# Normalizing and transposing the first layernorm's tokens in 32 by 32 blocks on VectorE instead of through TensorE

## The chip, the core and the metric

The kernel runs on one core of a Trainium2 chip. The metric is the device time of one execution in microseconds (us). Below, PE is TensorE's matmul stream, PEld its weight loads, DVE is VectorE, ACT is ScalarE, POOL is GpSimd, and SP is the engine that issues most DMAs. A DMA that is issued from SP, ACT or POOL stands in that engine's instruction stream, in order with its other instructions.

## What is computed

Four batches of 512 tokens with 512 features (x), and 1024 context rows for each batch. All numbers are float32.

```python
x = x + xattn(layernorm(x), ctx)     # linear attention, 16 heads of 32, feature map elu+1, sigmoid gate
x = x + moe(layernorm(x))            # 8 experts of 512x512, each token goes to its best 2

# layernorm: (x - mean) / sqrt(var + 1e-5) over the features, no scale or shift
# xattn:  q = f(query @ Wq.T); gate = sigmoid(query @ Wg.T + bg); k, v = split(kv @ Wkv.T); k = f(k)
#         out = ((q @ sum_s(k v)) / (q . sum_s(k) + 1e-6) * gate) @ Wo.T,  f(a) = a + 1 if a > 0 else exp(a)
# moe:    logits = x @ Wr; top 2; softmax over the two; sum of gate * (x @ We[e] + be[e])
```

The change concerns the first layernorm, the one ahead of the attention.

## The kernel before

Tokens come in tiles of 128 (`NT` = 4 for each batch), context rows in tiles of 128 (`NS` = 8 for each batch), and features in `NC` = 4 chunks of 128. A projection multiplies with the features on the 128 partitions, so the normalized tokens must be transposed: `xT` holds features on partitions and tokens along the row. For a tile, `normalized_T` (L248) normalizes into `xn` on DVE, and `transposed` (L241) makes four TensorE transposes of 128x128 into the PSUM tile `pt` and copies it to SBUF on ACT. The second layernorm's tokens (`row`, in `choose`, L471) go the same way into `x2T`, for the router's logits `pl`.

`layernorm_stats` (L225) makes mean and variance of each token with two DVE instructions for a tile, then the root on ACT and the reciprocal on DVE for four tiles at once. The result has a token on each partition.

The order of the work:

- `kv_tiles(b, lo, hi)` (L321) walks a batch's context tiles: for each, keys (`pk`: 8 matmuls; minimum on DVE, exponential on ACT, `k` by a second DVE instruction), values (`pv`: 8 matmuls, copied by ACT into `v`, whose last column a POOL memset fills with ones), and `kv_add`, which adds the tile before to the sums `kvs` (8 shorter matmuls). Two callbacks put other work in: `inside` after the first keys, `between` after each tile.
- Batch 0: three context tiles, the statistics of `x`, then five more, with `normalized_T` of one token tile between each of the first four.
- For each batch b: four projections for the queries (`pq`), with `dispatch(b - 1)` in the middle, then the gates (`pg`), the attention products (`pz`, `pn`), four context tiles of batch b + 1, the output projection (`po`, added to `x` on DVE), and the other four context tiles of batch b + 1. Between these last four, `normalized_T` of batch b + 1 and the next step of `choose(b)` take turns.
- `dispatch(b)` (L519) scatters each token's `row` to two places of the DRAM tensor `stream`, with eight indirect DMAs from POOL. Tokens are kept there by expert.
- Instead of a further batch, batch 3 has the first of the experts: `run` (L677) loads tiles of 128 rows from `stream` (`xg`, in blocks of 32 tokens by 128 features, four DMAs from SP, and `of`, two numbers for each token), transposes them 32 by 32 on DVE (`turned`, L721), multiplies (`pe`, 8 matmuls with one expert's weights), adds the bias into `y`, and scatters `y` to the DRAM tensor `result` (POOL, L757). Expert weights are loaded in this block layout too, so that a 32 by 32 transpose within partition groups is enough. 17 tiles are early ones and 18 late ones (steps 0 to 17; `SURE` = 18).
- At the steps of a plan (`begins`, `at_step`), `fetch` (L810) reads a token tile's rows of `result` back from POOL, `add` combines them with `x`, and `store` writes the output. The tiles fall in five groups; the first fetch of a group loads a row number into a register of POOL. The last two token tiles (14, 15) are read by SP and ACT after the last step.

The compiler's scheduler may reorder instructions of an engine within their dependencies. `tc.keep_in_program_order(i)` pins `i` behind the one instruction that was traced just ahead of it on its engine, and `mark()` (L455) writes a one-element tile on POOL with such a pin; successive marks also write the same bytes and so keep their order. A write to `result` is pinned behind its own mark. In `fetch`, the mark stands after the register load.

SP's loads are in program order. `cT` (context tiles) has three buffers, shared with `xg`; `row` has four, one for each token tile. `xT` is one buffer that each batch takes anew. `set_empty` fills `stream` with empty rows from SP, 1 MB at a time, during the first batches.

Of the kernel before, what the change touches and what calls it, by code (L numbers as in the profile page):

```python
# [9 lines left out]
F32 = mybir.dt.float32  # L10
# [3 lines left out]
ALU = mybir.AluOpType  # L14
# [3 lines left out]
P = 128  # L18
B, L, S, D = 4, 512, 1024, 512
E, F = 8, 512  # L20
HD = 32
NC = D // P
NT = L // P
NS = S // P
# [7 lines left out]
ROW = D + 2  # L32
# [7 lines left out]
SURE = LATE - 4  # L40
# [13 lines left out]
def xattn_moe_kernel(  # L54
# [14 lines left out]
    nc = tc.nc  # L69
# [9 lines left out]
    work = ctx.enter_context(tc.tile_pool(name="work", bufs=2))  # L79
    small = ctx.enter_context(tc.tile_pool(name="small", bufs=2))  # L80
    pmm = ctx.enter_context(tc.tile_pool(name="pmm", bufs=6, space=PSUM))
    pkv = ctx.enter_context(tc.tile_pool(name="pkv", bufs=1, space=PSUM))
    dram = ctx.enter_context(tc.tile_pool(name="dram", bufs=1, space=DRAM))
# [3 lines left out]
    result = dram.tile([NOWHERE + 2 * L, F], F32, name="result")  # L87


    def matmul(**operands):  # L90
        tc.keep_in_program_order(nc.tensor.matmul(**operands))  # L91

# [4 lines left out]
    latest = {}  # L97

    def load(dst, src):
        latest["load"] = nc.sync.dma_start(out=dst, in_=src)  # L100
        tc.keep_in_program_order(latest["load"])

    def load_ctx(b, s):
# [2 lines left out]
        load(t, cT[b, s])  # L106
        return t

    def load_x(b):
        tiles = []  # L110
        for t in range(NT):
            xt = xpool.tile([P, D], F32, tag="x", name=f"x_{b}_{t}")
            load(xt, x[b, t])
            tiles.append(xt)
        return tiles

    wkv_sb = wpool.tile([P, NC, 2 * D], F32, tag="wkv", name="wkv_sb")
    wq_sb = wpool.tile([P, NC, D], F32, tag="wq", name="wq_sb")
    wg_sb = wpool.tile([P, NC, D], F32, tag="wg", name="wg_sb")
    wo_sb = wpool.tile([P, NC, D], F32, tag="wo", name="wo_sb")  # L120
    wr_sb = wpool.tile([P, NC, E], F32, name="wr_sb")
    bg_sb = wpool.tile([P, NC], F32, name="bg_sb")


    we_sb = wpool.tile([P, E, NC, F], F32, name="we_sb")
    we_rows = we.rearrange("e (c f) i n -> e i f c n", f=HD)

# [14 lines left out]
    xs = {0: load_x(0)}  # L142

    turned = [(g, 0, g * HD, P - g * HD) for g in range(NC)]
    turned += [(g, P - g * HD, 0, g * HD) for g in range(1, NC)]
    wg_in = big.tile([P, NC, D], F32, tag="aT", name="wg_in")
    load(wg_in, wg)
    for g, a, b, n in turned:
        nc.gpsimd.tensor_copy(
            wg_sb[:, :, g * P + b : g * P + b + n], wg_in[:, :, g * P + a : g * P + a + n]  # L150
        )
        load(bg_sb[b : b + n, g : g + 1], bg[a : a + n, g : g + 1])
    load(wq_sb, wq)
    load(wr_sb, wr)
    for g, a, b, n in turned:
        load(wo_sb[b : b + n, g, :], wo[a : a + n, g, :])


    ident = const.tile([P, P], F32, name="ident")
# [18 lines left out]
    for g in range(NC):  # L178
        r = slice(g * HD, (g + 1) * HD)
        for i in range(NC):  # L180
            o = (i + g) % NC
            nc.gpsimd.affine_select(
                out=spread[r, o, :], in_=spread[r, o, :], pattern=[[0, HD]],
# [34 lines left out]
    def feature_map(dst, src):  # L218

        ex = work.tile([P, D], F32, tag="ex", name="ex")  # L220
        nc.vector.tensor_scalar(ex, src, 0.0, None, ALU.min)  # L221
        nc.scalar.activation(ex, ex, AF.Exp)  # L222
        nc.vector.scalar_tensor_tensor(dst, src, 0.0, ex, ALU.max, ALU.add)  # L223

    def layernorm_stats(tiles):  # L225
        mv = small.tile([P, NT, 2], F32, tag="mv", name="mv")
        for t in range(NT):
            st = small.tile([P, 6], F32, tag="st", name="st")
            nc.vector.bn_stats(st, tiles[t])
            nc.vector.bn_aggr(mv[:, t, :], st)  # L230
        rstd = small.tile([P, NT], F32, tag="rstd", name="rstd")
        nc.scalar.activation(rstd, mv[:, :, 1], AF.Sqrt, bias=eps_sb)
        nc.vector.reciprocal(rstd, rstd)
        return mv, rstd

    def normalize(dst, xt, t, mv, rstd):
        nc.vector.tensor_scalar(
            dst, xt, mv[:, t, 0:1], rstd[:, t : t + 1], ALU.subtract, ALU.mult
        )

    def transposed(dst, src):  # L241

        pt = pmm.tile([P, NC, P], F32, tag="mm", name="pt")
        for c in range(NC):
            transpose(pt[:, c, :], src[:, ts(c, P)])
        nc.scalar.copy(dst, pt)

    def normalized_T(xT, t, tiles, mv, rstd):  # L248

        xn = work.tile([P, D], F32, tag="ex", name="xn")  # L250
        normalize(xn, tiles[t], t, mv, rstd)
        transposed(xT[:, :, ts(t, P)], xn)

    def new_xT():
        return big.tile([P, NC, L], F32, tag="xT", name="xT")
# [199 lines left out]
    def mark():  # L455

        tc.keep_in_program_order(nc.gpsimd.memset(marked, 0.0))
# [13 lines left out]
    def choose(b, mv, rstd):  # L471

        pl = pmm.tile([P, NT, E], F32, tag="mm", name="pl")
        rows, xTs = [], []
        for t in range(NT):
            row = work.tile([P, ROW], F32, tag="row", name="row", bufs=NT)
            normalize(row[:, 0:D], xs[b][t], t, mv, rstd)
            nc.gpsimd.tensor_copy(row[:, D : D + 1], home[:, b * NT + t : b * NT + t + 1])
            rows.append(row)

        def logits(t):
            for c in range(NC):
                matmul(
                    out=pl[:, t, :],
                    lhsT=xTs[t][:, c, :],
                    rhs=wr_sb[:, c, :],
                    start=(c == 0),
                    stop=(c == NC - 1),
                )

        for t in range(NT):
            xTs.append(work.tile([P, NC, P], F32, tag="z", name="x2T"))
            transposed(xTs[t], rows[t])
            if t > 0:
                logits(t - 1)
            yield
        logits(NT - 1)
        lg = small.tile([P, NT, E], F32, tag="lg", name="lg")
        nc.vector.tensor_copy(lg, pl)

        def largest(name):
            m = small.tile([P, NT, 1], F32, tag=f"m{name}", name=f"m{name}")
            hot = small.tile([P, NT, E], F32, tag=f"hot{name}", name=f"hot{name}")
            at = small.tile([P, NT, 1], F32, tag=f"at{name}", name=f"at{name}")
            nc.vector.tensor_reduce(m, lg, AX.X, ALU.max)
            nc.vector.tensor_tensor(hot, lg, m.to_broadcast([P, NT, E]), ALU.is_equal)
            nc.vector.tensor_tensor(hot, hot, rank, ALU.mult)
            nc.vector.tensor_reduce(at, hot, AX.X, ALU.max)
            nc.vector.tensor_tensor(hot, hot, at.to_broadcast([P, NT, E]), ALU.is_equal)
            return m, hot, at  # L510

        m1, hot1, first = largest("1")
        nc.vector.scalar_tensor_tensor(lg, hot1, -BIG, lg, ALU.mult, ALU.add)
        m2, hot2, _ = largest("2")

        routed[b] = rows, m1, hot1, first, m2, hot2
        yield
# [292 lines left out]
    def fetch(t, tiles, queue, group=None):  # L810

        pool, tag = homes[t // 2 % len(homes)]
        if t not in fetched:
            pair = pool.tile([P, 2, 2, F], F32, tag=tag, name=f"y_{t}")
            fetched[t], fetched[t + 1] = pair[:, 0], pair[:, 1]
        if group is None:
            src = flat[:, t]
        else:
            if group not in rows_of:
                rows_of[group] = nc.values_load(  # L820
                    spots[0:1, group : group + 1], [queue.engine], min_val=0, max_val=NOWHERE,
                    skip_runtime_bounds_check_because="one of two constants",
                )
            row = rows_of[group] + (t - READ[group][0]) * 2 * P
            src = result[ds(row, 2 * P), :].rearrange("(p i) f -> p i f", i=2)
        mark()
        load = queue.dma_start(out=fetched[t], in_=src)
        behind(load, written["result"][:tiles], "results of the tokens")
        for put in written["result"][tiles:]:
            tc.declare_no_dep(load.ins, put.ins, reason=read_again)  # L830
        tc.keep_in_program_order(load)
        read_back.append(load)
# [31 lines left out]
    def plan(step, *what):  # L864
        at_step.setdefault(min(step, SURE), []).append(what)

    begins = (-3, -2, -1, 0, 5, 6, 7, 8, 10, 11, 14, 15, SURE - 1, SURE - 1)
    for g, (lo, hi, most) in enumerate(READ):
        for t in range(lo, hi):
            plan(begins[t], fetch, t, most, nc.gpsimd, g)  # L870
# [9 lines left out]

    xT = new_xT()
    kv_tiles(0, 0, 3)
    ln = layernorm_stats(xs[0])
    kv_tiles(0, 3, NS, lambda i: i < NT and normalized_T(xT, i, xs[0], *ln))
    kv_blocks(sums[0])
    for b in range(B):
        more = b + 1 < B
# [42 lines left out]
        next(product)  # L930
        if more:
            xs[b + 1] = load_x(b + 1)
            kv_tiles(b + 1, 0, NS // 2, inside=lambda: next(product))
        else:
            next(early)
            next(product)
            for _ in range(3):
                next(early)
        attention_out(b, aT)
        choice = choose(b, *layernorm_stats(xs[b]))  # L940
        if more:
            ln = layernorm_stats(xs[b + 1])
            xT = new_xT()

            def between(i):
                normalized_T(xT, i, xs[b + 1], *ln)
                next(choice)

            kv_tiles(b + 1, NS // 2, NS, between)
            next(choice)  # L950
            kv_blocks(sums[b + 1])
    for _ in range(2):
# [124 lines left out]
```

## Time and profile before

| what | value |
|---|---|
| median of 3 runs | 621.65 us (619.83 to 622.51) |
| profiled execution | 622.61 us, span 621.0 us |
| mean granted TensorE clock | 0.983 of full speed |
| PE / DVE / ACT / POOL busy | 588.5 / 271.0 / 115.2 / 100.6 us |
| DMA | 105.55 MB, 170 GB/s over the span |
| end of the last matmul | 597.3 us |

A line of instructions reads: source line, engine, operation, the tile written and the tiles read, shapes, and times. "L91" is the helper through which all matmuls go, "L94" the transposes, so groups are told apart by tile names. In a timeline a line has the start, the duration, the engine, and in brackets how long the engine sat idle before it and what ended that. In the list of an instruction's times the three numbers are the least, the median and the largest in ns. Matmuls are pipelined: their durations overlap, and starts tell how much of the stream one takes.

### The profile page before, as it was taken

What the parts mean: (1) busy time and instruction counts of PE and PEld (TensorE: products, weight loads), DVE (VectorE), ACT (ScalarE), POOL (GpSimd) and SP (SyncE); (2) the same over time, 40 slices, a digit from 0 to 9 for tenths busy, and PEclk for the clock granted to TensorE, in tenths of its full rate; (3) what the DMA queues carried; (4) which work ended last, traced back from release to release, by engine and by line L of the source; (5) the groups of instructions that cost most, each with busy time, mean ns of one, the idle gap of its engine ahead of it and who ended that gap; (6) DMA issues with size and microseconds to landing.
All of it is one profiled execution on the core that took longest, in us unless ns stands there. A gap on an engine that the chain in (4) does not pass through costs nothing. (4 is left out here: it accounts for less than half of the span.)

```text
span 621.0 us, 6578 instructions
## 1 busy us (share of the span) xinstructions
PE 588.5 (95%) x1908; PEld 286.3 (46%) x1908; DVE 271.0 (44%) x668; ACT 115.2 (19%) x180; POOL 100.6 (16%) x274
## 2 busy tenths in 40 slices
PE   7999999999999999999999999999999999999940
PEld 3555543454565335446643454565434554443410
DVE  2222243216215341351454226127874569475663
ACT  1322222112322221142222211322210100000000
POOL 4100000000002200000050000002311227455540
PEclk9999999999999999999999999999999999999985
DMA  8648920682686227527530660933344444889965
GB/s 317 191 158 301 293 81 2 167 240 69 164 248 184 81 86 237 153 85 221 186 137 1 203 204 0 327 130 137 116 114 119 96 119 177 262 243 259 296 219 173
DMA packets 68597, 105.55 MB, mean 170 GB/s; under 512 B 11981, under 2 KB 30413, under 8 KB 68176
## 3 DMA queue, kind: packets, MB, share of 16 engines
q1 hardware_dynamic: 58944, 76.24, 41.7%
q0 software_dynamic: 8176, 26.78, 12.1%
q10 hardware_dynamic: 1440, 2.10, 1.1%
q8 instruction: 16, 0.26, 0.2%
q14 instruction: 21, 0.17, 0.1%
HBM read 45.93 MB, written 59.94 MB: 170 GB/s over the span
## 5 line engine op out<-in xcount | busy, mean ns | idle before, releaser
L91 PE MATMUL pk<-wkv_sb,cT 128*128 128x512 f32 x256 | 118.6, 607 | 4.4 <-DMA cT<-in_cT_dram 4.4
L91 PE MATMUL pv<-wkv_sb,cT 128*128 128x512 f32 x256 | 115.2, 593 | 0.0
L221 DVE TENSOR_SCALAR ex<-pk 128x512 f32<-128x512 f32 x32 | 22.0, 688 | 148.3 <-PE pk L91 148.3
L91 PEld LDWEIGHTS pv<-wkv_sb,cT 128*128 128x128 f32 x256 | 48.4, 190 | 62.3 <-issue 59.3
L91 PEld LDWEIGHTS pk<-wkv_sb,cT 128*128 128x128 f32 x256 | 47.7, 194 | 57.8 <-issue 49.9
L91 PE MATMUL pe<-we_sb,xgT 128*128 x144 | 62.8, 595 | 0.6 <-DVE xgT L721 0.6
L91 PE MATMUL pe<-we_sb,turned_rows 128*128 x136 | 60.3, 597 | 0.7 <-DVE turned_rows L721 0.7
L278 POOL MEMSET v<- 128x4 f32 x32 | 3.3, 105 | 345.3 <-PE kvs L91 282.3
L91 PE MATMUL pg<-xT,wg_sb 128*128 128x512 f32 x128 | 56.7, 596 | 0.0
L91 PE MATMUL pq<-xT,wq_sb 128*128 128x512 f32 x128 | 56.6, 596 | 0.0
L91 PE MATMUL po<-wo_sb,aT 128*128 128x512 f32 x128 | 55.6, 592 | 0.0
L222 ACT ACTIVATE ex<-ex 128x512 f32<-128x512 f32 x48 | 30.2, 630 | 136.2 <-DVE ex L221 126.6
L757 POOL DMA_INDIRECT result<-y,to x35 | 35.8, 1023 | 93.7 <-DVE y L753 88.4
L91 PEld LDWEIGHTS pe<-we_sb,xgT 128*128 128x128 f32 x144 | 27.0, 190 | 36.3 <-issue 29.9
L91 PEld LDWEIGHTS pe<-we_sb,turned_rows 128*128 128x128 f32 x136 | 25.3, 190 | 32.4 <-issue 29.5
L563 POOL DMA_INDIRECT stream<-row,slot x32 | 31.9, 996 | 50.3 <-DVE cmp L591 22.5
L91 PEld LDWEIGHTS kvs<-v,k 128*128 128x128 f32 x256 | 33.3, 191 | 13.4 <-issue 13.4
L91 PEld LDWEIGHTS pg<-xT,wg_sb 128*128 128x128 f32 x128 | 24.0, 190 | 32.1 <-issue 32.1
L91 PEld LDWEIGHTS po<-wo_sb,aT 128*128 128x128 f32 x128 | 24.1, 190 | 29.2 <-issue 28.7
L91 PEld LDWEIGHTS pq<-xT,wq_sb 128*128 128x128 f32 x128 | 23.8, 190 | 27.3 <-issue 27.3
L91 PE MATMUL kvs<-v,k 128*128 128x129 f32 x256 | 34.0, 275 | 0.0
L223 DVE SCALAR_TENSOR_TENSOR k<-pk,ex 128x512 f32<-128x512 f32 x32 | 22.1, 690 | 19.5 <-ACT ex L222 19.5
(175 smaller groups left out, 465.1 us busy)
## 6 DMA issues: line engine op xcount, KB each, us to landing
stream<-empty SPq DMA_DIRECT2D x24, 1028.0 KB, 8.1
stream<-empty SPq DMA_DIRECT2D x8, 1285.0 KB, 6.8
xg<-stream SPq DMA_DIRECT2D x140, 64.0 KB, 2.7
we_sb<-in_we_dram SPq DMA_DIRECT2D x32, 256.0 KB, 5.5
cT<-in_cT_dram SPq DMA_DIRECT2D x31, 256.0 KB, 3.1
y<-result POOLq DMA_DIRECT2D x14, 512.0 KB, 5.5
x<-in_x_dram SPq DMA_DIRECT2D x16, 256.0 KB, 6.6
out_dram<-y POOLq DMA_DIRECT2D x10, 256.0 KB, 4.6
```

The lines of the kernel that those rows point to most:

```text
L91: tc.keep_in_program_order(nc.tensor.matmul(**operands))
L221: nc.vector.tensor_scalar(ex, src, 0.0, None, ALU.min)
L222: nc.scalar.activation(ex, ex, AF.Exp)
L223: nc.vector.scalar_tensor_tensor(dst, src, 0.0, ex, ALU.max, ALU.add)
L278: nc.gpsimd.memset(v[:, :, P : P + 1], 1.0)
L563: put = nc.gpsimd.indirect_dma_start(out=stream, out_offset=bass.IndirectOffsetOnAxis(ap=slots[i][:, t, :], axis=0), in_=rows[t], in_offse ...
L757: put = nc.gpsimd.indirect_dma_start(out=result, out_offset=bass.IndirectOffsetOnAxis(ap=home_i, axis=0), in_=y, in_offset=None, bounds_ch ...
```

## The change

The first layernorm's tokens are loaded a second time, in blocks (`load_blocks`): partition i x 32 + t holds, for each of the 16 groups of 32 tokens of a batch, the i-th 128 features of the group's token t. They are normalized in place, four DVE instructions of 128x128 for a token tile, and one DVE instruction transposes the tile 32 by 32 into `xT`. The weights `wq` and `wg` are loaded so that the feature order fits (`load_rows`, four DMAs instead of one). Mean and reciprocal root, which the statistics leave on the partitions of whole tokens, are written to the DRAM tensor `moments` by two POOL DMAs and read back to the blocks' partitions by four more (`spread_moments`). `tc.issue_after(latest["map"].ins)` queues the normalization on DVE behind the latest `k`.

The blocks take the buffer of the four `row` tiles, which become one tile of the same size. For batches 1 to 3 the statistics and the normalization move from the second four context tiles to the first four. `wo` is loaded after the first three context tiles instead of before them. In `fetch`, a `mark()` stands ahead of the register load, and token tiles 12 and 13 are read back at step `SURE - 2` instead of `SURE - 1`.

```diff
+    moments = dram.tile([B, HD, NT, P // HD, 2], F32, name="moments")
...
+    def load_blocks(b):
+        blocks = work.tile([P, NT, ROW], F32, tag="row", name="blocks", bufs=1)
+        blocks = blocks.rearrange("p t r -> p (t r)")[:, 0 : NT * D]
+        for i in range(NC):
+            load(
+                blocks[ts(i, HD), :].rearrange("t (n f) -> t n f", f=P),
+                x[b, :, :, ts(i, P)].rearrange("k (j t) f -> t (k j) f", t=HD),
+            )
+        return blocks
...
+    def load_rows(dst, w):
+        for i in range(NC):
+            load(dst[ts(i, HD)], w.rearrange("(c f) i n -> i f c n", f=HD)[i])
...
-    load(wg_in, wg)
+    load_rows(wg_in, wg)
...
-    load(wq_sb, wq)
+    load_rows(wq_sb, wq)
+    blocks = load_blocks(0)
     load(wr_sb, wr)
-    for g, a, b, n in turned:
-        load(wo_sb[b : b + n, g, :], wo[a : a + n, g, :])
...
-        nc.vector.scalar_tensor_tensor(dst, src, 0.0, ex, ALU.max, ALU.add)
+        latest["map"] = nc.vector.scalar_tensor_tensor(dst, src, 0.0, ex, ALU.max, ALU.add)
...
-    def normalized_T(xT, t, tiles, mv, rstd):
-        xn = work.tile([P, D], F32, tag="ex", name="xn")
-        normalize(xn, tiles[t], t, mv, rstd)
-        transposed(xT[:, :, ts(t, P)], xn)
+    def spread_moments(b, tiles):
+        mv, rstd = layernorm_stats(tiles)
+        for k, of in enumerate((mv[:, :, 0], rstd)):
+            nc.gpsimd.dma_start(
+                out=moments[b, :, :, :, k].rearrange("t n j -> j t n"), in_=of
+            )
+        ln = small.tile([P, NT, P // HD, 2], F32, tag="ln", name="ln", bufs=1)
+        for i in range(NC):
+            nc.gpsimd.dma_start(
+                out=ln[ts(i, HD)].rearrange("t n j k -> t (n j k)"),
+                in_=moments[b].rearrange("t n j k -> t (n j k)"),
+            )
+        return ln
+
+    def normalized_T(xT, t, blocks, ln):
+        rows = blocks[:, ts(t, D)].rearrange("p (j f) -> p j f", f=P)
+        with tc.issue_after(latest["map"].ins):
+            for j in range(P // HD):
+                nc.vector.tensor_scalar(
+                    rows[:, j], rows[:, j], ln[:, t, j, 0:1], ln[:, t, j, 1:2],
+                    ALU.subtract, ALU.mult,
+                )
+            nc.vector.transpose(
+                xT[:, :, ts(t, P)].rearrange("p c (j t) -> p j c t", t=HD),
+                rows.rearrange("p j (c f) -> p j c f", f=HD),
+            )
...
+        batch = work.tile([P, NT, ROW], F32, tag="row", name="rows", bufs=1)
         for t in range(NT):
-            row = work.tile([P, ROW], F32, tag="row", name="row", bufs=NT)
+            row = batch[:, t, :]
...
             if group not in rows_of:
+                mark()
                 rows_of[group] = nc.values_load(
...
-    begins = (-3, -2, -1, 0, 5, 6, 7, 8, 10, 11, 14, 15, SURE - 1, SURE - 1)
+    begins = (-3, -2, -1, 0, 5, 6, 7, 8, 10, 11, 14, 15, SURE - 2, SURE - 2)
...
     kv_tiles(0, 0, 3)
-    ln = layernorm_stats(xs[0])
-    kv_tiles(0, 3, NS, lambda i: i < NT and normalized_T(xT, i, xs[0], *ln))
+    for g, a, b, n in turned:
+        load(wo_sb[b : b + n, g, :], wo[a : a + n, g, :])
+    ln = spread_moments(0, xs[0])
+    kv_tiles(0, 3, NS, lambda i: i < NT and normalized_T(xT, i, blocks, ln))
...
             xs[b + 1] = load_x(b + 1)
-            kv_tiles(b + 1, 0, NS // 2, inside=lambda: next(product))
+            blocks = load_blocks(b + 1)
+            xT = new_xT()
+            def between(i):
+                if i == 0:
+                    ln.append(spread_moments(b + 1, xs[b + 1]))
+                else:
+                    for t in {1: (0,), 2: (1,), 3: (2, 3)}[i]:
+                        normalized_T(xT, t, blocks, ln[0])
+            ln = []
+            kv_tiles(b + 1, 0, NS // 2, between, inside=lambda: next(product))
...
         if more:
-            ln = layernorm_stats(xs[b + 1])
-            xT = new_xT()
-            def between(i):
-                normalized_T(xT, i, xs[b + 1], *ln)
-                next(choice)
-            kv_tiles(b + 1, NS // 2, NS, between)
+            kv_tiles(b + 1, NS // 2, NS, lambda i: next(choice))
```

## The prediction

> **What bounds the kernel now.** I read the page first: engine shares and the 40 slices.
>
> ```profile
> span 621.0 us, 6578 instructions
> ...
> PE 588.5 (95%) x1908; PEld 286.3 (46%) x1908; DVE 271.0 (44%) x668; ACT 115.2 (19%) x180; POOL 100.6 (16%) x274
> ...
> PE   7999999999999999999999999999999999999940
> ...
> PEclk9999999999999999999999999999999999999985
> ```
>
> TensorE is busy in every slice until the last two, at an unreduced clock; VectorE and ScalarE have room. So TensorE's stream sets when the tail begins, and what is taken out of it comes off one for one, if nothing new is late. Next the instructions on the tile pt, and TensorE's timeline in the second half of batch 1's context tiles.
>
> ```profile
> L94 PE MATMUL pt<-ident,xn x64: 272/273/328, 37.3 to 417.8; 128*128 128x128 f32 x64
> ...
> L246 ACT COPY xT<-pt x16: 586/586/587, 37.9 to 418.1; 128x512 f32<-128x512 f32 x16
> ```
>
> ```profile
> 147.14 3.60 PE L91 MATMUL pk<-wkv_sb,cT 128*128 128x512 f32 x8
> ...
> 154.00 1.06 PE L91 MATMUL kvs<-v,k 128*128 128x129 f32 x8
> 156.00 0.66 PE L94 MATMUL pt<-ident,xn 128*128 128x128 f32 x4 [0.94 <-DVE xn L237]
> 156.50 0.60 PE L94 MATMUL pt<-ident,row 128*128 128x128 f32 x4
> 156.93 3.60 PE L91 MATMUL pk<-wkv_sb,cT 128*128 128x512 f32 x8
> 160.37 3.60 PE L91 MATMUL pv<-wkv_sb,cT 128*128 128x512 f32 x8
> 163.80 1.06 PE L91 MATMUL kvs<-v,k 128*128 128x129 f32 x8
> 164.69 0.60 PE L94 MATMUL pt<-ident,xn 128*128 128x128 f32 x4
> 165.13 0.60 PE L94 MATMUL pt<-ident,row 128*128 128x128 f32 x4
> 165.57 0.96 PE L91 MATMUL pl<-wr_sb,x2T 128*128 128x8 f32 x8
> ```
>
> Matmuls overlap, so starts are what to subtract: the four transposes of a tile take 165.13 - 164.69 = 0.44 us of TensorE, not 4 x 0.27. And the first of them waits for its tile (bracket, 0.94); kvs to pt is 2.00 us where at 163.80 it is 0.89, so 1.11 us are lost. The same wait stands at 272.88 and 389.76. Last the end of the POOL timeline, and the chain that ended last.
>
> ```profile
> 592.02 0.55 POOL L851 DMA_DIRECT2D out_dram<-y  x1 [1.28 <-DVE y L840]
> ...
> 598.18 1.02 POOL L757 DMA_INDIRECT result<-y,to  x1 [0.27 <-DVEq L1012]
> ...
> 600.06 0.56 POOL L827 DMA_DIRECT2D y<-result  x1 [0.64 <-issue]
> ...
> 600.71 0.55 POOL L827 DMA_DIRECT2D y<-result  x1
> 604.72 1.03 POOL L757 DMA_INDIRECT result<-y,to  x1 [3.46 <-issue]
> ```
>
> ```profile
> 592.02 11.38 DMA out_dram<-y
> ...
> 604.72 2.33 DMA result<-y,to
> 607.30 6.38 DMA y<-result
> ```
>
> TensorE ends at 597.3; the last expert tile y is ready at 598.04, but its write leaves only at 604.72, after two reads that the program has behind it, and after the store of 592.02, the eighth POOL transfer before it, has landed (592.02 + 11.38 = 603.40). The last two read-backs start when that write has landed, at 607.05.
>
> **TensorE's part.** Sixteen tiles lose four transposes: 16 x 0.44 = 7.0 us, all in the full stream. The stall before the first transpose goes three times: 3 x 1.11 = 3.3, together 10.3. What is late next there is the transpose of row, now first. Its row (152.1 to 152.7 now, behind eight statistics) is behind four afterwards; TensorE asks at 154.9. No new stall. Checked by periods from pk to pk: the first is 156.93 - 147.14 = 9.79 and would be 7.75 + 0.44 = 8.19, so 1.60 less; the other three lose 0.44 each; three batches of 2.92 and batch 0's 4 x 0.44 make 10.5, which I take. ScalarE loses 16 copies of 0.59, off the path.
>
> By the Trainium skill, VectorE: DVE Perf Modes, The three transpose paths, one transpose of 128x128 (bf16) takes 390 ns on TensorE, and Rules for kernel authors gives such transposes to TensorE. By its 390 ns the 64 would save 25 us and the sum would read about 595; the rows here show 0.11 us each on the stream, and the trace decides.
>
> **VectorE's part.** A tile costs four subtract-and-scale on 128x128 and one transpose. The transpose of 128x512 is there: 0.70 (L721). 128x128 lies between 0.16 (L579, 128x4) and 0.54 (L237, 128x512): on the line between, 0.25. So 4 x 0.25 + 0.70 = 1.7 us a tile (1.3 to 2.9), against 0.54 removed. In the four first tiles of a batch (101.9 to 133.4) VectorE is busy 9.8 of 31.5 us; 4 x 1.7 and four statistics of 0.87 make it 20.1. Hidden, unless it waits.
>
> **The round trip over DRAM**, the open cost. After map(0) ends at 109.4, statistics 3.5, table load and root 1.28 + 0.30, reciprocal 0.17: moments ready at 114.7. POOL issues two writes of 512 four-byte runs; no such row is there. Bounds: 0.58 each (L827) to 4 x 0.97 = 3.9 (L563 has 128 rows); I take 1.0, since most of L563's 0.97 is shared by L827 with its larger rows. Landing: 3.2 (scatters of stream, 1.6 to 14.0). Four reads at 0.58 and a gap of 0.3: 3.6; landing 2.4 (of<-stream, 1.6 to 5.1). So ln lands at 114.7 + 2.0 + 3.2 + 3.6 + 2.4 = 125.9. The first normalization stands on VectorE behind map(1) (115.9) and waits; behind it stand the minimum, then the maximum, of k(2). The one waiting for those is kvs(2) at 132.5. Back from there 1.7 for the tile, 0.69 for the minimum, 0.76 for the exponential between, 0.69 for the maximum: ln must land by 128.7. Margin 2.8 us; each us beyond costs TensorE one us in each of three batches. Where the scheduler puts k(2) first, or the statistics into VectorE's idle 7.5 us before 101.2, the margin is larger. On POOL only the memset of v waits behind (118.19 now), used by the same kvs(2). I take nothing.
>
> The Trainium skill, DMA: Bandwidth & Descriptors, Specifications, holds that writes under 512 B become read-modify-writes, which speaks against these; its Anatomy of one DMA gives 2.0 us fixed for a POOL transfer. With 2.0 for both landings ln would be at 124.3; no run yet shows four-byte writes.
>
> **Loads.** Blocks are 1 MB a batch. At the start they replace wo's 1 MB in SP's order; six more weight loads and four block loads at some 0.45, less seven of wo (4.3 us), put cT(0,3) at 22.3 + 4.5 - 4.3 = 22.5. It lands 3.1 later (at most 5.0): 27.5, needed at 29.5. For batches 2 and 3 the block load waits on SP for the scatters of the batch before, whose rows share its buffer: the last leaves at 205.3, lands near 209. Behind it wait cT, expert weights and fills; the next cT is needed at 234.6, the blocks (8.9 at most for x, so 218) at about 232. Cost nothing; without that cover, one us per us. For batch 1 the load (68) falls into full DMA slices and has until 115. wo is needed at 133.
>
> **The tail.** With mark ahead of the register load, a write can no longer slip behind a group's first read; two reads move a step up. POOL's order becomes write 14, read 10, store, write 15, read 11, store, write 16, read 12, read 13, write 17. Read 12 waits until write 15 (595.6) lands at the median 3.9: 599.5; with register loads 0.9 and two issues, write 17 leaves at 601.6. The eighth transfer before it is now read 10 (about 593.9 + 5.5 = 599.4), done. Landing 3.9 (2.3 to 6.8): 605.5, against 607.05. Gain 1.5, between -1.4 and, if it could leave right behind write 16 at 599.3 and land in 2.3, 5.4.
>
> **Sum.** 10.5 + 1.5 = 12.0. The profiled execution took 622.61, 1.6 outside its span, so 610.6; it is 0.96 above the median 621.65, so the median becomes 609.7.
>
> **Rivals.** *Slower: the moments come too late.* If POOL pays by the descriptor (3.9 a write) and the reads land in 5.1, ln is at 114.7 + 7.8 + 3.2 + 3.6 + 5.1 = 134.4: 5.7 us too late, 3 x 5.7 = 17, time 627. It decides at a trip of 14.0 us; the gain is gone at 14.0 + 12.0/3 = 18.0; slower by 0.5% (3.1 us) from 19.0. For it: the margin is thin and landings reach 14.0. Against: short runs here (of, 8 bytes) land in 2.4. *Partly late:* 2 us three times, and no tail gain: 617. *The tail keeps its place or worse:* write 17 bound by the landing of write 15 at its longest 6.8: 611 to 612.5. *VectorE or SP becomes the bound at the start:* cT(0,3) late by up to 4: 614. *The stream does not shorten* (the compiler fills it with waits elsewhere): 621.
>
> **Numbers.** Forecast 0.65 (606 to 613), tail kept 0.08, start late 0.05, partly late 0.07: faster 0.85. Gain eaten by the trip or not there: 0.06. Late moments in full: 0.09. The range runs from about 605.7 (10.5 + 5.4 off) to 618 (10.5 off, tail -1.4 and 2 late in each of three batches: 618.5), leaving out some 0.15. About 0.5% is what a measurement of this kernel can tell from no change.
>
> **What would show it.** Right: no pt<-ident,xn; 9.0 us from pk to pk in the second half of a batch's tiles, 8.2 in its first; TensorE ending 10 us earlier; the last write of result some 3.5 us behind the one before (6.5 now), the last reads some 8 us behind TensorE's end instead of 10. Wrong: kvs waiting for k or v in tiles 1 to 3 of batches 1 to 3, VectorE idle on ln; pk waiting for cT near 30; a late write 17.

## The result, and where the time went

The changed kernel takes 625.98 us (median of 8 executions, 624.15 to 629.58) against 621.56 us for the kernel before (8 executions): ratio 1.0092, 95% interval 1.0074 to 1.0110. It is slower, by some 4.4 us in the medians; 609.7 was predicted. The profiled execution is one of the longer ones of its kernel (629.0 us, span 627.4). So below the trace tells where the time went, and the medians and ratios how much.

The page of the changed kernel, its shares and two of its rows in 40 slices (in this kernel's views L94 is the helper of all matmuls and L103 that of all loads from SP):

```profile
span 627.4 us, 6573 instructions
...
PE 583.6 (93%) x1844; PEld 280.3 (45%) x1844; DVE 291.0 (46%) x732; ACT 107.4 (17%) x164; POOL 122.5 (20%) x303
...
PE   7849999999999999999999999999999999998940
...
PEclk9959999999999999999999999999999999999985
```

TensorE has 64 matmuls less, as intended, but a hole in the third slice (31 to 47 us), and the granted clock falls there to half. After that it is at nine tenths or more up to the last two slices, as in the kernel before. Starts of landmarks on TensorE's timeline put the whole account in one table; pz is the first product of a batch's attention, so it comes once a batch.

| start of | before | after | difference | change since the row above |
|---|---|---|---|---|
| pz of batch 0 | 99.85 | 112.24 | +12.39 | +12.39 |
| pz of batch 1 | 216.73 | 226.21 | +9.48 | -2.91 |
| pz of batch 2 | 333.61 | 340.18 | +6.57 | -2.91 |
| pz of batch 3 | 450.71 | 454.37 | +3.66 | -2.91 |
| first pe from xgT (experts) | 533.91 | 537.55 | +3.64 | -0.02 |
| TensorE's end | 597.31 | 602.88 | +5.57 | +1.93 |
| end of the span | 621.0 | 627.4 | +6.4 | +0.83 |

The lines behind the first two rows, from the timelines of TensorE, before and then after, each with the fourth context tile's keys ahead of them:

```profile
29.53 3.60 PE L91 MATMUL pk<-wkv_sb,cT 128*128 128x512 f32 x8
...
99.85 1.14 PE L91 MATMUL pz<-z,spread 32*128 32x512 f32 x8
...
216.73 1.14 PE L91 MATMUL pz<-z,spread 32*128 32x512 f32 x8
```

```profile
40.67 6.58 PE L94 MATMUL pk<-wkv_sb,cT 128*128 128x512 f32 x8 [11.37 <-DMA cT<-in_cT_dram]
...
112.24 1.14 PE L94 MATMUL pz<-z,spread 32*128 32x512 f32 x8
...
226.21 1.14 PE L94 MATMUL pz<-z,spread 32*128 32x512 f32 x8
```

The gain is there, 2.91 us in each of three batches. It is paid away before the first pz, and a little more in the last two rows. The start, in the chain of waits of the changed kernel (start, duration, what):

```profile
11.70 7.94 DMA wg_in<-in_wg_dram
...
19.66 8.64 DMA wq_sb<-in_wq_dram
...
28.31 5.61 SPq L103
...
34.03 6.59 DMA cT<-in_cT_dram
...
40.67 6.58 PE pk L94 x8
```

The last piece of wg_in lands at 19.64, and only then does SP send the first piece of wq_sb; when that lands, at 28.30, SP goes on with wr_sb, whose issue takes 5.61 us; then cT(0,3), the fourth context tile, leaves, lands at 40.62, and the keys start. TensorE had stood idle for 11.37 us and then does the 8 matmuls in 6.58 us instead of 3.60. Together these are 14.35 us; less the 1.76 us of batch 0's transposes, 12.6, within 0.2 of the first row of the table.

Between the wg_in piece and wq_sb stand the seven loads of bg_sb; between the first piece of wq_sb and wr_sb stand three more pieces and four block loads. In both places a load left when the eighth load before it had landed, as if SP had eight places for loads under way. But the wait for a place is not all. SP's timeline in the changed kernel:

```profile
19.66 2.25 SPq L103 DMA_DIRECT2D wq_sb<-in_wq_dram  x4
21.95 5.63 SPq L103 DMA_DIRECT2D blocks<-in_x_dram  x4
28.31 5.61 SPq L103 DMA_DIRECT2D wr_sb<-in_wr_dram  x1
```

SP stood idle for only 0.73 us before wr_sb (27.58 to 28.31); longer were the issues themselves, 5.63 us for the four block loads and 5.61 for wr_sb. What holds SP inside an issue, the profile does not say. The profile before shows the wait for the eighth load too, in the timeline of SP:

```profile
9.46 0.33 SPq L100 DMA_DIRECT2D wg_in<-in_wg_dram  x1
10.14 4.87 SPq L100 DMA_DIRECT2D bg_sb<-in_bg_dram  x7
17.02 0.35 SPq L100 DMA_DIRECT2D wq_sb<-in_wq_dram  x1
```

SP stands still from 15.01 to 17.02; POOL's copies out of wg_in, which wait for its landing, start at 17.1. There it cost TensorE nothing: with it, and with 0.9 us of waiting for wq_sb behind it, cT(0,3) still left at 22.31, and the keys did not wait.

The DMA issues of the changed kernel (count, KB each, median us from issue to landing):

```profile
blocks<-in_x_dram SPq DMA_DIRECT2D x16, 256.0 KB, 10.1
...
ln<-moments POOLq DMA_DIRECT2D x16, 4.0 KB, 6.1
...
moments<-mv POOLq DMA_DIRECT2D x4, 2.0 KB, 9.6
...
moments<-rstd POOLq DMA_DIRECT2D x4, 2.0 KB, 13.8
```

The two writes of 2 KB in runs of four bytes take about as long as a block load of 256 KB, or longer. Batch 0's leave POOL at 18.23 and 20.12 us, into the stretch in which the weights are loaded.

### The profile page after: what moved, and what is told of

Read it like the earlier page. It is cut to its first block, busy times and chain, and to the rows that moved or that the text cites. A ratio compares the mean times of both kernels' runs of the same rounds, so it can differ in the third digit from the quotient of the medians.

```text
span 627.4 us, 6573 instructions
## 1 busy us (share of the span) xinstructions
PE 583.6 (93%) x1844; PEld 280.3 (45%) x1844; DVE 291.0 (46%) x732; ACT 107.4 (17%) x164; POOL 122.5 (20%) x303
## 4 chain that ended last, share of the span: by engine, by line
PE 76%; DMA 12%; DVE 4%; SPq 3%; issue 3%; POOL 1%; ACTq 0%; DVEq 0%; POOLq 0%; ACT 0%
PE pk L94 17%; PE pv L94 16%; PE pg L94 9%; PE pq L94 9%; PE po L94 9%; PE pe L94 7%; PE kvs L94 4%; DMA xg<-stream 4%; DMA cT<-in_cT_dram 3%; PE pl L94 2%; DMA result<-y,to 2%; SPq L746 2%; DMA wq_sb<-in_wq_dram 1%; PE pn L94 1%; DMA wg_in<-in_wg_dram 1%
## 5 line engine op out<-in xcount | busy, mean ns | idle before, releaser
L94 PE MATMUL pk<-wkv_sb,cT 128*128 128x512 f32 x256 | 121.1, 618 | 15.8 <-DMA cT<-in_cT_dram 15.8
L94 PE MATMUL pv<-wkv_sb,cT 128*128 128x512 f32 x256 | 115.2, 593 | 0.0
L94 PEld LDWEIGHTS pk<-wkv_sb,cT 128*128 128x128 f32 x256 | 48.6, 198 | 70.8 <-issue 51.8
L94 PEld LDWEIGHTS pv<-wkv_sb,cT 128*128 128x128 f32 x256 | 48.4, 190 | 62.4 <-issue 59.9
L94 PE MATMUL pe<-we_sb,xgT 128*128 x144 | 62.8, 594 | 2.6 <-DVE xgT L763 2.6
L94 PE MATMUL pe<-we_sb,turned_rows 128*128 x136 | 60.3, 597 | 0.7 <-DVE turned_rows L763 0.7
L94 PE MATMUL pg<-xT,wg_sb 128*128 128x512 f32 x128 | 56.7, 595 | 0.0
L94 PE MATMUL pq<-xT,wq_sb 128*128 128x512 f32 x128 | 56.6, 596 | 0.0
L94 PE MATMUL po<-wo_sb,aT 128*128 128x512 f32 x128 | 55.6, 592 | 0.0
L799 POOL DMA_INDIRECT result<-y,to x35 | 36.1, 1031 | 91.4 <-DVE y L795 89.8
L94 PEld LDWEIGHTS pe<-we_sb,xgT 128*128 128x128 f32 x144 | 27.1, 190 | 38.1 <-issue 31.8
L605 POOL DMA_INDIRECT stream<-rows,slot x32 | 32.0, 1000 | 53.5 <-DVE mv L248 22.6
L94 PEld LDWEIGHTS pe<-we_sb,turned_rows 128*128 128x128 f32 x136 | 25.3, 190 | 32.4 <-issue 29.5
L94 PEld LDWEIGHTS kvs<-v,k 128*128 128x128 f32 x256 | 33.3, 191 | 13.5 <-issue 13.4
L94 PEld LDWEIGHTS pg<-xT,wg_sb 128*128 128x128 f32 x128 | 24.0, 190 | 32.1 <-issue 32.1
L94 PEld LDWEIGHTS po<-wo_sb,aT 128*128 128x128 f32 x128 | 24.1, 190 | 29.2 <-issue 28.7
L94 PEld LDWEIGHTS pq<-xT,wq_sb 128*128 128x128 f32 x128 | 23.8, 190 | 27.3 <-issue 27.3
L94 PE MATMUL kvs<-v,k 128*128 128x129 f32 x256 | 34.0, 275 | 0.0
```

The lines of the kernel that those rows point to most:

```text
L605: put = nc.gpsimd.indirect_dma_start(out=stream, out_offset=bass.IndirectOffsetOnAxis(ap=slots[i][:, t, :], axis=0), in_=rows[t], in_offse ...
L799: put = nc.gpsimd.indirect_dma_start(out=result, out_offset=bass.IndirectOffsetOnAxis(ap=home_i, axis=0), in_=y, in_offset=None, bounds_ch ...
```

## The experiments

Three edits could have delayed cT(0,3): the six more weight loads, the four-byte writes, and the block loads ahead of it. Each was cured or added alone and together. The times stand against the kernel before on the same chip; comparisons between experiments go by these ratios, and places and waits by one profiled execution of each.

**e1, the writes made coarser.** One write of 128 runs of 32 bytes in place of two of 512 runs of 4.

```diff
-        for k, of in enumerate((mv[:, :, 0], rstd)):
-            nc.gpsimd.dma_start(out=moments[b, :, :, :, k].rearrange("t n j -> j t n"), in_=of)
+        nc.vector.tensor_copy(mv[:, :, 1], rstd)
+        nc.gpsimd.dma_start(out=moments[b].rearrange("t j n k -> j t (n k)"),
+                            in_=mv.rearrange("p n k -> p (n k)"))   # moments is [B, HD, P // HD, NT, 2]
...                                                                      # ln and its reads likewise
```

> The changed kernel, but mean and reciprocal root stand side by side, so that each batch writes its moments with one POOL transfer of 128 runs of 32 bytes instead of two of 512 runs of 4 bytes. Theory CLOG: the 4-byte writes hold the DMA engines (8 to 14 us to land, 0 to 27 GB/s on the whole chip side while they run), and the weight, block and context loads issued behind them land late. Expected: the write lands within 4 us, wq and blocks within 6 to 8 us, TensorE waits less than 2 us for the fourth context tile (11.4 in the changed kernel) and keeps its clock; 612 to 614 us. Theory LANES: SP keeps only eight loads in flight and waits until the eighth before has landed, so the number of loads is what counts. Expected: the wait for the fourth context tile stays above 8 us; 622 to 626. Theory SLOW BLOCKS: the 512-byte runs of the block load are what is slow: 622 to 626.

Measured: 621.06 us (10 runs), ratio 0.9978 (0.9964 to 0.9993). cT(0,3) leaves at 28.62, TensorE waits 3.75 us, the first pz comes at 104.46. From the write's issue to the reads it is 21.3 to 28.9 us, where the changed kernel takes 18.23 to 34.36. The writes' form is worth 7.8 us of the start.

**e2, the weights in one load each.** The order of the features is made by the layout in which wq and wg are handed to the kernel; nothing else moves. Each row of a load then is one run of 8 KB, where the pieces had runs of 2 KB.

```diff
-    load_rows(wg_in, wg)
+    load(wg_in, wg)
-    load_rows(wq_sb, wq)
+    load(wq_sb, wq)
-        return w.T.reshape(NC, P, -1).transpose(1, 0, 2)
+        return w.T.reshape(NC, NC, HD, -1).transpose(0, 2, 1, 3).reshape(P, NC, -1)   # wq, wg alone
```

> The changed kernel, but wq and wg lie in the block order in DRAM already, so each is one load of 128 rows of 8 KB instead of four of 32 partitions. The load of the fourth context tile then is the 14th behind wg's instead of the 20th. LANES: the load leaves SP near 23 to 25 us instead of 34, TensorE waits under 2 us; 612 to 614 us. CLOG: the load leaves earlier but lands with everything else when the 4-byte writes are through, near 31 to 35 us; TensorE waits 3 to 7 us; 617 to 622. SLOW BLOCKS: as CLOG, but the moments' writes land fast.

Measured: 615.09 us (4 runs), ratio 0.9880 (0.9857 to 0.9903). cT(0,3) leaves at 23.00, TensorE waits 2.52 us, the first pz comes at 101.69. With the slow writes still in it, the kernel is faster than before. The pieces are worth 10.6 us of the start.

**e3, the block loads behind the first three context tiles.**

```diff
-    blocks = load_blocks(0)
     load(wr_sb, wr)
...
     kv_tiles(0, 0, 3)
+    blocks = load_blocks(0)
```

> The changed kernel, but batch 0's blocks are loaded behind the first three context tiles' loads instead of ahead of them. SLOW BLOCKS: TensorE waits under 2 us for the fourth context tile; 612 to 614 us. CLOG: that tile's load is issued some 5 to 8 us sooner, but lands with the 4-byte writes near 31 to 35 us; TensorE waits 2 to 7 us; 616 to 622. LANES: four loads fewer ahead of it, so it leaves SP near 28 when the first of wq's loads has landed; TensorE waits 3 to 6 us; 616 to 620.

Measured: 622.99 us (10 runs), ratio 1.0003 (0.9989 to 1.0017). cT(0,3) leaves at 23.27, 10.8 us earlier than in the changed kernel, but now takes 13.85 us to land; TensorE waits 7.82 us, the first pz comes at 108.83. The place on SP was not all: the load itself was slow, beside whatever was under way with it.

**e4, the kernel before with batch 0's two four-byte writes added**, which nothing reads.

```diff
+    moments = dram.tile([B, HD, NT, P // HD, 2], F32, name="moments")
...
     ln = layernorm_stats(xs[0])
+    for k, of in enumerate((ln[0][:, :, 0], ln[1])):
+        nc.gpsimd.dma_start(out=moments[0, :, :, :, k].rearrange("t n j -> j t n"), in_=of)
```

> The kernel before, and besides the two 4-byte writes of batch 0's moments to DRAM, which nobody reads; nothing else is changed. CLOG: they take 8 to 14 us to land, the bytes moved between 19 and 30 us fall, and the fourth context tile, issued near 22.3 as before, lands 5 to 10 us later than before, so that TensorE waits 3 to 8 us, with the clock reduced after it: 625 to 632 us. LANES and SLOW BLOCKS: two small transfers more; 621 to 622.5.

Measured: cT(0,3) leaves at 22.63 (22.3 before), TensorE waits for nothing, the first pz comes at 100.14. In this execution the writes by themselves do not hold up the start. But it is the fastest of the eight (623.04 us); the median is 625.83 us, ratio 1.0047 (1.0028 to 1.0065), which lies where CLOG put it. Where the other executions lose it is open.

None of the three theories holds alone: coarser writes (e1) and fewer loads (e2) each take away more than half of the delay, the later block loads (e3) take away 3.4 us, and the writes alone (e4) make little of it. The next expectations add a fourth, LANES WITH A SLOW TRIP: the slow writes and the number of loads do harm together.

**e8, the kernel before with wq and wg in four pieces of 32 partitions; e10, the same with e4's writes.**

```diff
-    load(wg_in, wg)
+    for i in range(NC):
+        load(wg_in[ts(i, HD)], wg[ts(i, HD)])       # wq_sb likewise; e10: and the two writes of e4
```

These pieces have runs of 8 KB, those of the change runs of 2 KB, so that only the splitting is tried here.

> The kernel before, with wq and wg loaded in four pieces of 32 partitions each as in the change, and nothing else. LANES alone (SP keeps eight loads in flight, so six loads more delay the fourth context tile): that tile's load leaves SP at 25 to 28 us instead of 22.3 and lands at 29 to 32; TensorE waits 0 to 3 us; 621.5 to 625. LANES WITH A SLOW TRIP (the loads' number only hurts while the 4-byte writes make each landing late): the load leaves by 25 and TensorE does not wait; 621 to 622.5.

> As the last one, and besides the two unread 4-byte writes of batch 0's moments. LANES alone: as the last one, within 1 us. LANES WITH A SLOW TRIP: wq's pieces land 4 to 8 us later than in the last one, the fourth context tile's load leaves SP 4 us later, TensorE waits 3 to 8 us and runs its next eight matmuls at a reduced clock; 626 to 632.

Measured: e8 takes 625.97 us (8 runs), ratio 1.0072 (1.0050 to 1.0094); e10 634.32 us (4 runs), ratio 1.0208 (1.0174 to 1.0242), beyond the 632 expected at most. The fourth keys on TensorE's timeline, first of e8 and then of e10 (in brackets the idle time before, and what ended it):

```profile
31.57 5.40 PE L91 MATMUL pk<-wkv_sb,cT 128*128 128x512 f32 x8 [2.91 <-DMA cT<-in_cT_dram]
```

```profile
38.31 6.39 PE L93 MATMUL pk<-wkv_sb,cT 128*128 128x512 f32 x8 [8.56 <-DMA cT<-in_cT_dram]
```

And how long a piece of wq_sb was under way, in the DMA issues of e8 and of e10:

```profile
wq_sb<-in_wq_dram SPq DMA_DIRECT2D x4, 256.0 KB, 4.5
```

```profile
wq_sb<-in_wq_dram SPq DMA_DIRECT2D x4, 256.0 KB, 10.2
```

And SP's waits for these pieces (us in total, times, longest), again e8 and then e10:

```profile
SPq L100 <- DMA wq_sb<-in_wq_dram: 1.7, 3, 0.9
```

```profile
SPq L102 <- DMA wq_sb<-in_wq_dram: 5.8, 4, 1.8
```

This shows the main cause. These two kernels keep the old layernorm, without blocks and without the tail's edits, and yet e10 loses 11.57 us up to the first pz. The writes alone lose 0.29 and the pieces alone 3.84; their sum, 4.13, is far below what they lose in one kernel. The writes make the pieces slow (4.5 to 10.2 us; 11.8 in the changed kernel). In e10 the pieces hand the delay on to cT(0,3) through SP's eight places: of the 5.6 us by which that load leaves later than in e8, 4.1 are SP's longer waits for the pieces. In the changed kernel this wait is the smaller part, 0.73 us; there the slow issues of the block loads and of wr_sb (11.2 us together, 5.5 in e12 below and 6.3 in e1) hand it on, and why they are slow is not shown. The meeting stands in the times too, if smaller: e4 and e8 lose 0.47% and 0.72%, 1.19% together, e10 2.08%, and the ends of their intervals, 1.59% and 1.74%, do not touch.

Counted so in these profiles, against 99.85 (or 98.09 where the transposes are gone), the changed kernel's start is late by 14.15 us: 0.29 by the writes, 3.84 by the pieces, 7.44 by their meeting, and 2.58 by the rest, of which the block loads are the largest new item. The terms overlap, so the order in which they are counted matters.

**e9, both cures (e1 and e2); e6, and the blocks later too (e3).**

> The changed kernel with both cures: moments in one transfer of 32-byte runs, and wq and wg in one load each. One load each alone left a wait of 2.5 us for the fourth context tile and one slow row of matmuls, 32-byte runs alone 3.8. LANES WITH A SLOW TRIP: the wait and the slow row go (4 to 4.5 us of TensorE's stream); 610.5 to 613. If the 512-byte block loads, still ahead of that tile, hold it up by themselves: a wait of 2 us stays; 614 to 616.

> The last one, and batch 0's blocks loaded behind the first three context tiles' loads. The fourth context tile's load has no block load ahead of it and leaves near 19. Every theory: TensorE does not wait for it; TensorE's stream is 10.5 us shorter than before by the time the experts start; 610 to 612.5, the rest being the tail. If it is within 0.5 of the last one, the block loads' place costs nothing.

Measured: e9 613.59 us (4 runs), ratio 0.9878 (0.9835 to 0.9921), TensorE waits for no cT, the first pz at 96.85. e6 614.61 us (4 runs), ratio 0.9900 (0.9868 to 0.9932), no wait, the first pz at 97.93. Both are a little slower than expected. The block loads may stay where the change put them, once the other two are cured; and most of the change's gain on TensorE reaches the end.

**e12, the meeting avoided in time.** The changed kernel with all its loads and four-byte writes, but batch 0's moments copied behind the third tile's keys, so that the writes leave POOL at 28.55 us; batch 0's normalizations move behind later tiles.

```diff
+        if b == 0:
+            with tc.issue_after(latest["map"].ins):
+                for k in range(2):
+                    nc.vector.tensor_copy(held[:, k], of_both[k])      # the two writes take held
...
-    kv_tiles(0, 3, NS, lambda i: i < NT and normalized_T(xT, i, blocks, ln))
+    kv_tiles(0, 3, NS, between0)     # tiles 0 and 1 at i == 2, tile 2 at 3, tile 3 at 4
```

> The changed kernel, all its loads and its four-byte writes kept, but batch 0's moments copied on VectorE behind the keys of the third context tile (some 28 us) and written from the copies, so that the two writes leave POOL some 10 us later than in the changed kernel (near 29 instead of 19 us); batch 0's normalizations stand behind the sixth to eighth context tile. LANES WITH A SLOW TRIP (the slow writes and the many weight loads hurt each other because they are under way together): by 29 us SP has sent the weights, so cT(0,3) leaves SP near 27, as in the kernel before with split loads (27.27), TensorE waits some 3 us for it instead of 11.4, the first pz is near 102 to 104 instead of 112, and the time is some 616 to 618. If the six more loads and the block loads alone, or what is loaded at all, make the delay, cT(0,3) leaves at 34 as before, the first pz stays near 112 and the time near 626. A third way: the late writes meet the block and context loads, ln lands after 55 us, and VectorE stops behind the sixth tile: cT(0,3) early, but an idle stretch of TensorE near 60, time up to 622.

Measured, in the chain of waits of e12:

```profile
20.89 4.01 DMA wq_sb<-in_wq_dram
24.92 3.44 SPq L103
28.47 5.37 DMA cT<-in_cT_dram
```

The first piece of wq_sb lands in 4.01 us instead of 8.64, cT(0,3) leaves 5.6 us earlier, TensorE waits 4.85 us instead of 11.37, and the first pz comes at 105.12 instead of 112.24. VectorE does not stop for ln. The time is 621.65 us (11 runs), ratio 0.9976 (0.9952 to 1.0000): 1.2% below the changed kernel's ratio, some 7 us, as much as the pz. 616 to 618 was expected; the start is still 7.0 us late, where the pieces alone, in e8, made 3.8.

**e5, e7 and e11, the tail.** e5 is the changed kernel without its two tail edits, e7 the kernel before with them alone, e11 is e9 without them.

```diff
             if group not in rows_of:
-                mark()
                 rows_of[group] = nc.values_load(
...
-    begins = (-3, -2, -1, 0, 5, 6, 7, 8, 10, 11, 14, 15, SURE - 2, SURE - 2)
+    begins = (-3, -2, -1, 0, 5, 6, 7, 8, 10, 11, 14, 15, SURE - 1, SURE - 1)
```

> The changed kernel with its two edits of the tail undone: the register load again ahead of its mark, token tiles 12 and 13 read back one step later. TAIL HELPS (the prediction's 1.5 us): the last write of result leaves later than in the changed kernel, the time is some 627.5 against its 626.0. TAIL DOES NOTHING: 626. TAIL COSTS: the waits that the changed kernel has between its first expert transposes and its last matmul (65.3 us there, 63.4 in the kernel before) go back to some 63.4, and the time is 624.5; about 0.5 us of it either way by where the last write lands. The start is as in the changed kernel in all three: the first pz near 112.

> The kernel before with the two edits of the tail alone. TAIL HELPS: 620.0 against 621.5, the last write leaving 3 us earlier, right behind the reads of tiles 12 and 13. TAIL DOES NOTHING: 621.5. TAIL COSTS: expert stage (first transposes to last matmul) 65 us instead of 63.4, tail as before, time 623.

> The changed kernel with one load for each of wq and wg, moments in one write of runs of 32 bytes, and the two edits of the tail undone. Without the tail's undoing it took 613.6. TAIL HELPS: 615. TAIL DOES NOTHING: 613.6. TAIL COSTS: 612, with the expert stage at 63.4 us instead of 66.6. If the stage stays at 65 or more, what lengthens it is not the tail's edits but something else of the change.

Measured: e5 624.77 us (11 runs), ratio 1.0037 (1.0017 to 1.0057); e7 623.08 us (11 runs), ratio 1.0011 (0.9995 to 1.0028); e11 613.40 us (4 runs), ratio 0.9862 (0.9839 to 0.9885). The edits gain in none of the three pairs; against the changed kernel e5 is better by some 3 us, of which its trace puts 1.2 before the first pz (111.06), where the edits have no part; in the other two pairs no difference can be told. POOL's timeline at the end of the changed kernel, and the last write in its chain of waits:

```profile
606.60 0.55 POOL L870 DMA_DIRECT2D y<-result  x1
...
607.50 1.02 POOL L799 DMA_INDIRECT result<-y,to  x1 [0.27 <-issue]
```

```profile
607.50 5.67 DMA result<-y,to
```

The same write in the chains of e7 (with the edits) and of e5 (without):

```profile
603.51 6.06 DMA result<-y,to
```

```profile
606.89 2.32 DMA result<-y,to
```

| from TensorE's end to | before | e5 | e11 | after | e7 | e9 |
|---|---|---|---|---|---|---|
| the tail edits | no | no | no | yes | yes | yes |
| last write leaves | 7.4 | 6.9 | 6.9 | 4.6 | 5.2 | 3.8 |
| SP's last read-back starts | 10.0 | 9.5 | 9.4 | 10.5 | 11.5 | 10.7 |

With the edits the write leaves two to three us earlier, and the read-back that waits for it starts about one us later. It now leaves within a microsecond of two reads of 512 KB, and takes 5.7 to 6.1 us in these two chains (5.1 in e3, 4.9 in e12) where it took 2.3. That it shares the DMA engines with these reads is the likely reading; it was not tried apart. The stretch from the first expert matmuls on xgT to TensorE's end is 63.1 to 66.6 us in the eight kernels with the edits and 62.1 to 64.4 in the six without, one profile each: they overlap, and e11 is at 64.4 without the edits, so what lengthens it is not settled.

## Why the prediction was wrong

**TensorE's part was right.** 10.5 us were taken out as forecast: 2.92 for a batch, 2.91 measured three times; batch 0 from its fourth keys to pz takes 70.32 us before and 71.57 after, which without the 2.98 us of slow matmuls is 1.73 less (1.76 forecast). The first period of the second four tiles of batch 1 is 8.19 us (159.53 to 167.72), as forecast. No matmul of pt from xn is left, and no new stall of row's transposes. In the first four tiles of batch 1 the period from keys to keys is 7.75 us, undisturbed (TensorE's timeline of the changed kernel):

```profile
130.28 3.60 PE L94 MATMUL pk<-wkv_sb,cT 128*128 128x512 f32 x8
...
138.03 3.60 PE L94 MATMUL pk<-wkv_sb,cT 128*128 128x512 f32 x8
```

**VectorE's part was right.** A tile takes 1.11 us for four instructions of 128x128 and 0.71 for the transpose, 1.8 against the 1.7 taken, and no wait of TensorE ends with it.

**The step that failed is "Loads"**, the term that "put cT(0,3) at 22.3 + 4.5 - 4.3 = 22.5" with a landing of at most 5.0, and booked it at nothing. It left at 34.03 and landed 6.59 later. The sum added issue times as if SP were limited by issuing alone, at 0.45 us each. The six more pieces alone, in e8, put cT(0,3) 4.96 us later, and in the changed kernel the block loads took 5.63 us to issue and wr_sb 5.61. The sum also missed that a load waits for the eighth one before it to land, although SP's idle stretch before wq_sb at 17.02 lay in the profile before, and although the same prediction's tail reckons with "the eighth POOL transfer before it". It also gave the pieces no longer landing than the load they replaced, and put the round trip's writes, costed two paragraphs earlier for their own sake, nowhere beside them. The rival "cT(0,3) late by up to 4" named the right place; the wait and the slow matmuls after it cost 14.35, and its chance of 0.05 was too small.

**The round trip was mis-sized too, and luck covered it.** The prediction took 1.0 us for issuing a write, 3.2 for its landing and 2.4 for the reads', 11.2 in all, against a limit of 14.0. The rows show 1.6 to 2.0, 9.6 and 13.8, and 6.1: in batch 1 the moments are ready at 89.8 and the reads leave POOL only at 106.26, 16.5 us later and not yet landed. That is past the limit where the rival begins. It cost nothing (no wait of TensorE ends with ln or xT): the scheduler had put the statistics of batches 1 to 3 into the query stage (batch 1's from 84.94 on, instead of from the 109.4 assumed), a way out that the prediction only mentioned. The landing was also read from the wrong rows: "1.6 to 14.0" is of all transfers on stream, fills and loads too; the scatters alone (L563) take 2.8 to 4.4, and the four-byte writes took 6.6 to 15.3. The price of this term showed up elsewhere, as the slow landing of wq_sb in batch 0.

**The tail's 1.5 us did not come.** POOL's order is the one foreseen, and the write leaves 4.6 us after TensorE's end where 4.3 was forecast. What failed is the landing: 3.9 was taken from a row that mixes the writes of result with its read-backs (the writes alone, L757, have 3.4 in the median, 6.3 at most), 5.67 came, behind two reads that the same edit puts right ahead of it.

Two sections of one page bear on this. In the Trainium skill, DMA: Bandwidth & Descriptors, Rules for kernel authors says that transfers to disjoint partition halves serialize and advises one transfer over 128 partitions. Here it was quarters; e2 and e8 agree with the advice: the pieces cost the kernel before 3.84 us of its start and the changed kernel 10.6. The same page's Anatomy of one DMA gives a POOL transfer 2.0 us fixed; the four-byte writes, at 9.6 and 13.8 us, are far from it in this case.

The version that beats both kernels is the changed one with one load for each weight, wq and wg handed over in block order, and runs of 32 bytes: 613.6 us (e9), and 613.4 without the tail edits (e11), 1.2 to 1.4% below the kernel before. The spans of these profiles are 612.1 and 610.1 against 621.0, that is 8.9 and 10.9 less.

## What to carry to other kernels

At this kernel's start the loads were a queue with eight places: when one load is split, count not only its issues but whose landing each later load will now wait for, down to the first one that TensorE needs. A small transfer can cost little alone and much through what it slows, so put a new transfer on the same time axis as every other one under way, in particular those that a queue waits for. And when a write is moved earlier to end a wait, look at what it will land beside.

## What the runs showed of the hardware

- TensorE's granted clock answers to short idle stretches. In the changed kernel it is 0.50 from 38 to 44 us, around the end of 11.37 us of idle; but already after 2.52 us (e2) and 2.91 us (e8) the next 8 matmuls take 5.40 us instead of 3.60, at a mean clock of 0.67 in both. The timeline of e2:

```profile
31.30 5.40 PE L94 MATMUL pk<-wkv_sb,cT 128*128 128x512 f32 x8 [2.52 <-DMA cT<-in_cT_dram]
```

  The Trainium skill, TensorE: Matmul & The Clock Gate, What's actually happening, puts the fall to half clock after an idle window of about 3.4 us; here a shorter wait was enough, and it added 1.80 us to its own 2.52.
- Moments in one write of 32-byte runs took POOL 0.79 us to issue (e1) and 7.7 us to land (e9, median), against 1.63 and 1.99 us, 9.6 and 13.8 us for the two of four-byte runs with the same numbers.
- The issue of wr_sb, a short load, took 0.42 and 0.43 us where no block loads stood right ahead of it (e8, e3) and 2.1 to 5.6 us where they did (e9, e2, e12, e1 and the changed kernel). What SP waits for inside that issue the profile does not resolve; it stays open.
